# A first norm by sums and squares, a copied column pair, one more tile, stores in three parts and a new priority table in a four-layer graph kernel

## The chip, the cores and the metric

The kernel runs on one core of one Trainium2 chip. Its time is the device time of one execution in microseconds (us). The hardware profiler's span, from the first to the last instruction, stands beside it where a profile was taken. The engines are TensorE (PE: matmuls, transposes; PEld is its loading of weights, which overlaps PE), VectorE (DVE), ScalarE (ACT), GpSimd (POOL) and SyncE (SP, which here only issues DMAs).

## The reference, cut to what matters

Sixteen graphs of 1024 nodes with 128 features (float32) go through four layers. Each layer ends with `x = layernorm(x + layer(x))`.

```
x = layernorm(x + L0(x, adj))   # softmax over the mask adj^T, two weight products, two batch norms over ALL graphs
x = layernorm(x + L1(x, adj))   # h = x W + b; s1 = h a1; s2 = h a2; e = leaky_relu(s1_i + s2_j + b_a);
                                # softmax over i under the mask; relu(attention @ h)
x = layernorm(x + L2(x, adj))   # scores leaky_relu((x*a) x^T) under the mask, softmax, alpha @ x
x = layernorm(x + L3(x, adj))   # the same with other weights
```

Layer 0 needs statistics over all graphs. After that the graphs ("batches" here, 0 to 15) don't touch each other.

## The kernel before, in words

**Two stages.** The first stage streams all adjacency matrices once for the matrix products of layer 0 and its batch norms. It leaves a 128x1024 intermediate per batch in DRAM (`people`), a row sum per node (`srow`), a 128x128 matrix `m`, and two constant rows (`shift2_rows`, `row_rows`). The second stage does the rest for each batch: the end of layer 0 (called part 0), the attention layer (part 1) and the two relation layers (parts 2 and 3). After it a small check ends in a branch past a general path that isn't run.

**The second stage is a list of operations that a planner orders** (`Plan`, and `steps` from L885). A batch is a list of 389 operations (387 after the change). Each has an engine, an assumed cost, the things it reads and writes, and perhaps a tile that it takes from a class. `run` gives each operation the key `BEGIN[batch][part] + WHEN[number in the batch]`, sorts all of them by it, and places them in this order. An operation whose inputs aren't placed yet, or whose class has no free tile, is held, and goes in as soon as it can, lowest key first. The order of placing is the order of each engine's instructions. So the tables say who goes first on an engine; they are no times.

**What limits the order.** There are three lanes: batch b uses the tiles of lane b mod 3, so batch b+3 can't begin where batch b still reads. Classes: two PSUM banks (`bank`, 128x512) for transposes, small products and results; three wide PSUM tiles (`big`, 128x1024) for scores and for the accumulator of part 1; four `p`, two `e`, two `u` and two `u2` tiles in SBUF; six tiles `a` for blocks of the adjacency matrix; one `yn` and one `x0`.

**Chunks and groups.** A batch's 1024 rows are 8 chunks of 128. Row groups g0, g1, g2 hold 4, 3 and 1 chunks (`GROUPS`).

**Part 0** (L1011 to L1040): load `yn` from `people` and `x0` from `x`. DVE adds `shift2_rows` to all of `x0` (L1015, one 128x1024 instruction) and `row_rows * srow` to each chunk (L1018, eight). For each group PE transposes `yn` (L984), ACT copies it to `xt` (L997), PE multiplies by `m` into a bank (L1027), DVE adds bank and `x0` into the lane's rows (L1035, one instruction a group). `collect` then takes `bn_stats` and `bn_aggr` of each chunk on DVE (L910, L912), and `norm` computes the scale on POOL (L922, L602, L603, L924) and applies it on ACT (L928).

**Part 1**: the rows are transposed again; for 3, 3 and 2 chunks (`heads`, L1060) PE multiplies `xt` by `w1a`, which has 130 columns: h, then s1 and s2. ACT makes three exponentials from the last two columns while they are in the bank (L1064 `r`, L1068 twice into `ucol`), DVE adds the bias to h (L1071, into `hn`, which lies in the tile `q`). When all `ucol` are there, PE transposes them (L1076), ACT copies the result (L1079), SP stores it to DRAM (L1081) and loads it back, spread over all partitions, as `u` and `u2` (L1082). Eight times (j = 0..7) DVE then makes weights from `u`, `u2`, `r` (L1095) and masks and sums them (L1098), takes a reciprocal (L1102), ACT scales `hn` (L1104), PE accumulates (L1110). L1117 adds the residual and sums the row on DVE (`accum_out`), ACT squares and sums (`collect1`, L934), POOL and ACT normalize (`norm1`, L946 to L954).

**Parts 2 and 3**, for each chunk c: scores on PE into a `big` tile (L1160) and transposes of blocks done already (L1174); ACT makes two exponentials (L1182 into `q`, L1186 into an `e` tile); DVE takes the greater (L1189) and masks (L1197, L1201); PE multiplies by the rows (L1210, into a bank); DVE divides and adds (L1215, L1219); ACT squares (L961), POOL and ACT normalize (L972, L973, L977). Last, SP stores all 8 chunks of the batch by one DMA (L1228, 512 KB).

`edges` (L1006) is the load of a block of the adjacency matrix; `scores3 c`, `prod1 j` and the like below mean the scores of part 3 for chunk c, the product of part 1 for j.

Of the kernel before, what the change touches and what calls it, by code (L numbers as in the profile page):

```python
# [8 lines left out]
F32 = mybir.dt.float32  # L9
# [3 lines left out]
ALU = mybir.AluOpType  # L13
# [3 lines left out]
P = 128  # L17
# [33 lines left out]
    (0, 23570, 19046, 19887),  # L51
    (81560, 99857, 99273, 99605),
    (180283, 179933, 178976, 179336),
    (260846, 259630, 259039, 259785),
    (340425, 339643, 339400, 340684),
    (420530, 420135, 420071, 421111),
    (501099, 500913, 500796, 501932),
    (581571, 581330, 581585, 582255),
    (662316, 662119, 661973, 662851),
    (743065, 742561, 742499, 743453),  # L60
    (823698, 823225, 823027, 824059),
    (903448, 903617, 903689, 904441),
    (983901, 984234, 984054, 984182),
    (1064533, 1064511, 1063640, 1064017),
    (1145623, 1144421, 1143836, 1144698),
    (1225002, 1224181, 1224938, 1228420),
)
WHEN = (
    0, 616797, 620532, 622095, 622948, 622949, 623081, 627024, 628364, 629540, 630002, 626714,
    631822, 632733, 637162, 643567, 643568, 646286, 646287, 641291, 643860, 640736, 645808, 649097,  # L70
    651067, 652419, 650894, 651816, 622197, 623918, 623919, 635538, 637455, 638511, 638209, 638511,
    637940, 638511, 638512, 648524, 653255, 649232, 641328, 648299, 658881, 661110, 661111, 661112,
    662588, 667230, 666632, 667775, 666734, 667975, 667627, 668167, 670412, 673075, 673098, 672381,
    672546, 670025, 673246, 672675, 672066, 671126, 668971, 669586, 670331, 668972, 669567, 673463,
    673491, 673492, 676047, 679090, 680801, 664034, 688211, 689909, 692376, 693478, 693479, 687926,
    698241, 698991, 700751, 700752, 701641, 698697, 705538, 707234, 707621, 709778, 709779, 708998,
    712153, 715144, 717643, 718560, 721467, 716887, 726655, 728125, 729013, 731234, 733170, 717089,
    733625, 734320, 736822, 737034, 740401, 724366, 743419, 743865, 744720, 745329, 745637, 738233,
    746339, 748381, 750352, 751241, 751242, 757138, 760265, 754447, 757472, 756401, 757315, 759434,
    759855, 767039, 768190, 768045, 768169, 767040, 759823, 765592, 758156, 766635, 758407, 760720,  # L80
    773599, 776709, 777039, 776774, 755717, 755829, 763757, 763758, 770613, 775993, 775974, 777040,
    785094, 777064, 771978, 776750, 777256, 769200, 777666, 777741, 777742, 784114, 783251, 785781,
    786534, 787453, 791218, 791573, 800503, 779418, 782258, 784827, 784828, 785903, 787585, 788060,
    789078, 790147, 791144, 792926, 797796, 797797, 797798, 782555, 787352, 789581, 790841, 791385,
    792274, 793488, 795097, 800473, 804195, 805111, 805112, 788539, 791008, 792740, 794006, 793572,
    796652, 797265, 797266, 798162, 800436, 803200, 804120, 814202, 817329, 814870, 814589, 814203,
    791642, 794100, 796952, 796953, 796953, 799319, 799479, 800939, 806609, 809130, 809131, 814876,
    792024, 797770, 800401, 802811, 803071, 803570, 804913, 806406, 811328, 811329, 812948, 813716,
    793459, 798927, 804482, 804483, 804483, 808047, 809552, 810259, 814079, 814543, 814544, 816050,
    818957, 822320, 822707, 822318, 792793, 800025, 810709, 810918, 810710, 810919, 810920, 811403,  # L90
    815213, 816668, 818414, 818900, 820448, 823067, 817639, 818248, 819205, 822769, 824203, 823188,
    823787, 827042, 823788, 800843, 823673, 824102, 824833, 827370, 826533, 827423, 830962, 834981,
    837327, 843714, 851180, 804761, 821610, 824915, 826767, 828740, 831819, 828941, 832181, 833942,
    835127, 838612, 843863, 844088, 846801, 815635, 824848, 834898, 834899, 834899, 836257, 840309,
    840766, 840767, 846958, 848086, 852097, 822209, 824988, 836352, 838893, 838981, 841309, 845130,
    845131, 847798, 848858, 851129, 860560, 873534, 885192, 935009, 874885, 874459, 823674, 828798,
    842035, 842354, 842429, 846335, 847385, 848026, 848027, 854821, 855402, 871955, 823537, 839881,
    847114, 847115, 847497, 848712, 854653, 854822, 855246, 859637, 861054, 874928, 827895, 845561,
    848713, 854472, 854936, 855954, 857288, 858683, 859934, 865640, 867594, 875036, 878161, 933277,
    890148, 907626, 830840, 852078, 855955, 859901, 858372, 861853, 863289, 863508, 871434, 874384,  # L100
    874817, 875044, 909812, 957303, 971916,
# [453 lines left out]
def fast_path(ctx, tc, x, adj, adjt, k1, k2, w1, vecs, b_w, b_a, out, bad):  # L555
# [293 lines left out]
    class Lane:  # L849


        def __init__(self, i):
# [12 lines left out]
            self.st = tile([P, C, 6], "st")  # L865
            self.sq = tile([P, C], "sq")
            self.total = tile([P, C], "total")
            self.mv = [tile([P, C, 2], f"mv{k}") for k in range(2)]
            self.rstd = [tile([P, C], f"rstd{k}") for k in range(2)]
            self.off = [tile([P, C], f"off{k}") for k in range(2)]  # L870
            self.r = tile([P, C], "r")
            self.ucol = tile([P, 2, C], "ucol")
# [5 lines left out]
    for cls, n in (("u", 2), ("u2", 2), ("p", 4), ("e", 2)):  # L878
        plan.tiles(cls, [lanes.tile([P, N], F32, name=f"f_{cls}{i}") for i in range(n)])
# [6 lines left out]
    def steps(b):  # L886
# [20 lines left out]

        def collect(v, c):

            op(DVE, 0.2, lambda: nc.vector.bn_stats(ln.st[:, c, :], ln.rows[v][:, c, :D]),  # L910
               [key(f"rows{v}", c)], [key("st", c)], late=TAIL)
            op(DVE, 0.09, lambda: nc.vector.bn_aggr(ln.mv[v][:, c, :], ln.st[:, c, :]),  # L912
               [key("st", c)], [key(f"mv{v}", c)], late=TAIL)

        def norm(v, g):

            t, mv, rstd, off = ln.rows[v], ln.mv[v], ln.rstd[v], ln.off[v]

            def scales():
                n = len(group(g))  # L920
                neg = small.tile([P, 4], F32, name="f_ln_neg")
                nc.gpsimd.tensor_scalar(neg[:, :n], mv[:, chunks(g), 0], -1.0, 1.0, ALU.mult, ALU.mult)  # L922
                rsqrt(rstd[:, chunks(g)], mv[:, chunks(g), 1], LN_EPS, n)
                nc.gpsimd.tensor_tensor(off[:, chunks(g)], neg[:, :n], rstd[:, chunks(g)], ALU.mult)  # L924

            op(POOL, 2.0, scales, keys(f"mv{v}", group(g)), [key(f"scale{v}", g)], late=0.1)
            for c in group(g):
                op(ACT, 0.4, lambda c=c: nc.scalar.activation(  # L928
                    t[:, c, :D], t[:, c, :D], AF.Identity, bias=off[:, c:c + 1],
                    scale=rstd[:, c:c + 1]), [key(f"scale{v}", g)], [key(f"rows{v}", c)], late=TAIL)  # L930
# [72 lines left out]
        def edges(s, src):  # L1003
# [11 lines left out]
        op(DVE, 1.15, lambda t: nc.vector.tensor_tensor(  # L1015
            t, t, shift2_rows[:, None, :].to_broadcast([P, C, D]), ALU.add), mods=[x0])
        for c in range(C):
            op(DVE, 0.21, lambda t, c=c: nc.vector.scalar_tensor_tensor(  # L1018
                t[:, c, :], row_rows, srow[:, b * C + c:b * C + c + 1], t[:, c, :], ALU.mult, ALU.add),
                mods=[x0], late=TAIL if c == C - 1 else 0.0)  # L1020
        for g in range(len(GROUPS)):
            pt = turn(lambda c, t: t[:, c, :], [], g, ["xt"], args=[yn])
            copied(pt, g, ln.xt, "xt")

            def product(t, g=g):
                for k, c in enumerate(group(g)):
                    nc.tensor.matmul(t[:, k * P:(k + 1) * P], ln.xt[:, c * P:(c + 1) * P], m,  # L1027
                                     start=True, stop=True)

            pp = op(PE, 0.2235 * len(group(g)), product, [key("xt", g)], keys("rows0", group(g)),  # L1030
                    take="bank", late=0.2)

            def add(t, u, g=g, y=y):
                n = len(group(g))
                nc.vector.tensor_add(y[:, chunks(g), :D], t[:, :n * D].rearrange("p (k d) -> p k d", d=D),  # L1035
                                     u[:, chunks(g), :])

            op(DVE, 0.1 + 0.124 * len(group(g)), add, [], keys("rows0", group(g)), args=[pp, x0], late=TAIL)
            for c in group(g):
                collect(0, c)  # L1040
            norm(0, g)
# [10 lines left out]
        for c0 in range(0, C, 3):  # L1052
# [5 lines left out]
            def heads(t, c0=c0, n=n, view=view):  # L1058
# [5 lines left out]
            op(ACT, 0.15, lambda t, c0=c0, n=n, view=view: nc.scalar.activation(  # L1064
                ln.r[:, c0:c0 + n], view(t)[:, :, D], AF.Exp, bias=k0, scale=-(1 - SLOPE)),
# [237 lines left out]
```

## Time and profile before

| what | us |
|---|---|
| median of 3 runs (lowest to highest) | 1713.57 (1713.35 to 1716.01) |
| the profiled execution's own time | 1715.12 |
| its span | 1713.2 |
| PE busy in the span | 1615.4 (94%) |
| DVE busy | 1325.4 (77%) |
| ACT busy | 1071.7 (63%) |
| POOL busy | 338.3 (20%) |
| mean granted TensorE clock | 0.984 |

The profile's page gives the busy share of each engine in 40 slices of 42.8 us. The first ten slices are the first stage. Around 425 to 450 us lies the passage from the first stage to the second; from about 510 us three batches are always in work, until about 1600 us; then the last batches run out. Other views list, for one engine and a stretch of time, what it waited for, or all its instructions in order of time. A matmul of float32 shows as two records. PE's records overlap (pipelining), so a row's mean duration is longer than the pace: the 16 records of one product L1210 take 1.79 us in the chain of work.

### The profile page before, as it was taken

The numbers are of one execution on the slowest core, as the hardware profiler recorded it, in microseconds if no ns is written. First come the engines' busy times: TensorE is split into PE (matmuls) and PEld (weight loads), VectorE is DVE, ScalarE is ACT, GpSimd is POOL, SyncE is SP. The second block draws the span as 40 slices with busy tenths as digits, with TensorE's granted clock in tenths as the row PEclk, the third lists the DMA queues.
The fourth block names the chain that finished last, engine by engine and source line by source line (L and its number), as shares of the span: only waits on it lengthen the run. The fifth ranks groups of instructions, "written<-read, shape, count | busy, mean of one in ns | idle before, by whom it ended". The sixth has DMA issues, their size and how long they took to land. (4 is left out here: it accounts for less than half of the span.)

```text
span 1713.2 us, 34530 instructions
## 1 busy us (share of the span) xinstructions
PE 1615.4 (94%) x13023; PEld 1447.6 (84%) x13023; DVE 1325.4 (77%) x2940; ACT 1071.7 (63%) x2703; POOL 338.3 (20%) x615
## 2 busy tenths in 40 slices
PE   6999999999469999999999999999999999999996
PEld 3666666666469999999999999999999999999995
DVE  4665565565658989898888989898898989888764
ACT  6555555642245667767676776767677676767663
POOL 0000000000222132313313242231324232231310
PEclk9999999999789999999999999999999999999998
DMA  8999999996355757676666766766676677667551
GB/s 306 381 368 391 359 370 395 357 391 251 133 161 174 206 168 218 202 214 205 204 200 185 222 198 209 212 197 203 188 215 198 206 210 209 192 178 209 177 157 52
DMA packets 394641, 397.14 MB, mean 232 GB/s; under 512 B 10592, under 2 KB 339168, under 8 KB 394464
## 3 DMA queue, kind: packets, MB, share of 16 engines
q1 hardware_dynamic: 377824, 386.45, 69.4%
q10 hardware_dynamic: 16640, 8.39, 1.6%
q8 instruction: 104, 1.70, 0.4%
q14 instruction: 73, 0.60, 0.1%
HBM read 377.89 MB, written 16.91 MB: 230 GB/s over the span
## 5 line engine op out<-in xcount | busy, mean ns | idle before, releaser
L1210 PE MATMUL f_pbank<-f_rows,f_p 128*128 128x129 f32 x4096 | 498.9, 275 | 1.7 <-ACT f_xt L997 1.0
L1210 PEld LDWEIGHTS f_pbank<-f_rows,f_p 128*128 128x128 f32 x4096 | 478.3, 192 | 2.9 <-ACT f_xt L997 1.4
L1160 PE MATMUL f_pbig<-f_xt,f_hw 128*128 128x128 f32 x2304 | 303.9, 277 | 3.5 <-ACT f_hw L999 2.5
L1160 PEld LDWEIGHTS f_pbig<-f_xt,f_hw 128*128 128x128 f32 x2304 | 281.2, 192 | 4.8 <-ACT f_hw L999 3.0
L1110 PE MATMUL f_pbig<-f_q,f_p 128*128 128x128 f32 x2048 | 257.7, 280 | 19.0 <-ACT f_q L1104 19.0
L1189 DVE TENSOR_TENSOR f_q<-f_q,f_e 128x1024 f32<-128x1024 f32 (+7 forms) x256 | 193.4, 756 | 101.4 <-ACT f_q L1182 62.9
L1182 ACT ACTIVATE f_q<-f_pbig,f_neg_shift 128x1024 f32<-128x1024 f32 (+7 forms) x256 | 189.1, 739 | 130.3 <-PE f_pbig L1174 125.6
L1110 PEld LDWEIGHTS f_pbig<-f_q,f_p 128*128 128x128 f32 x2048 | 246.0, 197 | 21.3 <-ACT f_q L1104 20.9
L1186 ACT ACTIVATE f_e<-f_pbig,f_neg_shift 128x1024 f32<-128x1024 f32 (+7 forms) x256 | 188.4, 736 | 58.5 <-PE f_pbig L1174 53.6
L1197 DVE TENSOR_TENSOR f_p<-f_q,f_a 128x1024 f32<-128x1024 f32 (+7 forms) x256 | 192.1, 750 | 2.2 <-issue 0.2
L739 PE MATMUL f_pz<-f_xs,f_at 128*128 128x390 bf16 x1024 | 180.4, 331 | 5.0 <-DVE f_xs L722 4.2
L739 PE MATMUL f_pz<-f_zs,f_att 128*128 128x390 bf16 x1024 | 181.0, 328 | 3.1 <-DVE f_yf L742 2.9
L760 ACT ACTIVATE f_junk<-f_at,f_sq_bias 128x1024 bf16<-128x1024 int32 x128 | 146.9, 1148 | 51.6 <-DVE f_yf L742 48.2
L1095 DVE SCALAR_TENSOR_TENSOR f_p<-f_u,f_r,f_u 128x1024 f32<-128x1024 f32 x128 | 162.7, 1271 | 2.1 <-DMA f_u<-f_u_dram 2.0
L739 PEld LDWEIGHTS <-f_at 128*128 128x128 fp8e4 x1024 | 100.5, 98 | 74.1 <-issue 7.6
L739 PEld LDWEIGHTS <-f_att 128*128 128x128 fp8e4 x1024 | 100.0, 98 | 69.6 <-issue 6.5
L1098 DVE SCALAR_TENSOR_TENSOR f_p<-f_p,f_a 128x1024 f32<-128x1024 f32 x128 | 155.7, 1216 | 0.8
L1201 DVE TENSOR_TENSOR f_p<-f_pbig,f_a 128x128 f32<-128x128 f32 (+6 forms) x224 | 151.9, 678 | 0.0
L742 DVE TENSOR_REDUCE f_zr<-f_pz 128x129 f32<-128x387 f32 x128 | 63.2, 553 | 113.4 <-PE f_pz L739 113.3
L1174 PE MATMUL f_pbig<-f_ident,f_q 128*128 128x128 f32 x896 | 135.8, 274 | 3.5 <-DVE f_q L1189 3.3
L972 POOL TENSOR_SCALAR f_ln_var<-f_sq 128x3 f32<-128x3 f32 (+2 forms) x96 | 35.9, 374 | 506.1 <-ACT f_junk L961 506.1
L997 ACT COPY f_xt<-f_pbank 128x512 f32<-128x512 f32 (+2 forms) x192 | 83.2, 441 | 71.6 <-PE f_pbank L984 71.5
(165 smaller groups left out, 2075.4 us busy)
## 6 DMA issues: line engine op xcount, KB each, us to landing
f_a<-in_adjt_dram SPq DMA_DIRECT2D x384, 512.0 KB, 4.7
f_at<-in_adj_dram SPq DMA_DIRECT2D x64, 1024.0 KB, 9.1
f_att<-in_adjt_dram SPq DMA_DIRECT2D x64, 1024.0 KB, 13.5
f_u<-f_u_dram SPq DMA_DIRECT2D x32, 512.0 KB, 6.4
f_xn<-in_x_dram SPq DMA_DIRECT2D x16, 512.0 KB, 11.3
f_people<-f_yf ACTq DMA_DIRECT2D x16, 512.0 KB, 16.8
f_yn<-f_people SPq DMA_DIRECT2D x16, 512.0 KB, 3.8
f_x<-in_x_dram SPq DMA_DIRECT2D x16, 512.0 KB, 6.6
```

The lines of the kernel that those rows point to most:

```text
L739: nc.tensor.matmul(pz[:, :3 * K], a8[:, j % 2, c * 512:(c + 1) * 512:4], moving[:, j].rearrange("p k d -> p (k d)"), start=(j == 0), stop= ...
L760: nc.scalar.activation(junk, at[c // 2][:, c % 2, :], AF.Square, bias=sq_bias, accum_out=squares[:, b, c:c + 1])
L1095: p = op(DVE, 1.2, lambda e, t, t2, *_, j=j: nc.vector.scalar_tensor_tensor(e, t2, ln.r[:, j:j + 1], t, ALU.mult, ALU.max), [key("r", j)], ...
L1098: op(DVE, 1.24, lambda t, e, j=j: nc.vector.scalar_tensor_tensor(e, e, 1.0, t.rearrange("p c n -> p (c n)"), ALU.mult, ALU.mult, accum_out ...
L1110: nc.tensor.matmul(t[:, c * D:(c + 1) * D], q[:, c * P:(c + 1) * P], hn[:, j, :], start=False, stop=(j == C - 1 and c % 4 == 3))
L1160: nc.tensor.matmul(t[:, j * P:(j + 1) * P], hw[:, j * P:(j + 1) * P], xt[:, mine], start=True, stop=True)
L1182: nc.scalar.activation(q[:, blocks, :], t[:, c * P:].rearrange("p (c n) -> p c n", n=P), AF.Exp, bias=neg_shift)
L1186: nc.scalar.activation(e[:, c * P:], t[:, c * P:], AF.Exp, bias=neg_shift, scale=SLOPE)
L1189: nc.vector.tensor_max(q[:, blocks, :], q[:, blocks, :], e[:, c * P:].rearrange("p (c n) -> p c n", n=P))
L1197: nc.vector.tensor_mul(t[:, c * P:].rearrange("p (c n) -> p c n", n=P), q[:, blocks, :], k[:, c:, :])
L1201: nc.vector.tensor_mul(t[:, :c * P].rearrange("p (c n) -> p c n", n=P), s[:, :c * P].rearrange("p (c n) -> p c n", n=P), k[:, :c, :])
L1210: nc.tensor.matmul(t[:, :D + 1], w[:, j * P:(j + 1) * P], xl[:, j, :], start=(j == 0), stop=(j == C - 1))
```

## The change

It has five parts.

1. **First norm.** `collect` and `norm` are gone. In part 0 the addition of bank and `x0` is now one `scalar_tensor_tensor` per chunk with `accum_out` (the row's sum), and `collect1` and `norm1`, which part 1 used already, square and normalize. The addition of `shift2_rows` is made by group, just ahead of the group's rows.
2. **Columns of the heads.** ACT copies both columns of each `heads` bank into a new small tile `s12` (three copies), and the three exponentials are made once each from `s12` for all 8 chunks. The transpose L1076 now waits for the two whole `ucol` exponentials.
3. **Three `e` tiles** instead of two.
4. **Output by row groups**: three DMAs of 256, 192 and 64 KB per batch, each after its group is normalized.
5. **New tables** `BEGIN` and `WHEN`.

```diff
-    for cls, n in (("u", 2), ("u2", 2), ("p", 4), ("e", 2)):
+    for cls, n in (("u", 2), ("u2", 2), ("p", 4), ("e", 3)):
...
-        op(DVE, 1.15, lambda t: nc.vector.tensor_tensor(
-            t, t, shift2_rows[:, None, :].to_broadcast([P, C, D]), ALU.add), mods=[x0])
-        for c in range(C):
-            op(DVE, 0.21, lambda t, c=c: nc.vector.scalar_tensor_tensor(
-                t[:, c, :], row_rows, srow[:, b * C + c:b * C + c + 1], t[:, c, :], ALU.mult, ALU.add),
-                mods=[x0], late=TAIL if c == C - 1 else 0.0)
...
-            op(DVE, 0.1 + 0.124 * len(group(g)), add, [], keys("rows0", group(g)), args=[pp, x0], late=TAIL)
+            op(DVE, 0.07 + 0.134 * len(group(g)), lambda t, g=g: nc.vector.tensor_tensor(
+                t[:, chunks(g), :], t[:, chunks(g), :],
+                shift2_rows[:, None, :].to_broadcast([P, len(group(g)), D]), ALU.add), mods=[x0])
             for c in group(g):
-                collect(0, c)
-            norm(0, g)
+                op(DVE, 0.21, lambda t, c=c: nc.vector.scalar_tensor_tensor(
+                    t[:, c, :], row_rows, srow[:, b * C + c:b * C + c + 1], t[:, c, :], ALU.mult, ALU.add),
+                    mods=[x0], late=TAIL)
+            for k, c in enumerate(group(g)):
+                op(DVE, 0.3, lambda t, u, k=k, c=c, y=y: nc.vector.scalar_tensor_tensor(
+                    y[:, c, :D], t[:, k * P:(k + 1) * P], 1.0, u[:, c, :], ALU.mult, ALU.add,
+                    accum_out=ln.total[:, c:c + 1]), [], [key("rows0", c), key("total", c)], args=[pp, x0],
+                    late=TAIL)
+                collect1(0, c)
+            norm1(0, g)
...
-            op(ACT, 0.15, lambda t, c0=c0, n=n, view=view: nc.scalar.activation(
-                ln.r[:, c0:c0 + n], view(t)[:, :, D], AF.Exp, bias=k0, scale=-(1 - SLOPE)),
-                [], keys("r", range(c0, c0 + n)), args=[ph], late=TAIL)
-            for k in range(2):
-                op(ACT, 0.15, lambda t, k=k, c0=c0, n=n, view=view: nc.scalar.activation(
-                    ln.ucol[:, k, c0:c0 + n], view(t)[:, :, D + 1], AF.Exp, scale=SLOPE ** k),
-                    [], [key("ucol", k, c0)], args=[ph], late=TAIL)
+            op(ACT, 0.15, lambda t, c0=c0, n=n, view=view: nc.scalar.copy(
+                ln.s12[:, c0:c0 + n, :], view(t)[:, :, D:D + 2]), [], [key("s12", c0)], args=[ph], late=TAIL)
...
+        for k in range(2):
+            op(ACT, 0.15, lambda k=k: nc.scalar.activation(
+                ln.ucol[:, k, :], ln.s12[:, :, 1], AF.Exp, scale=SLOPE ** k), s12, [key("ucol", k)],
+                late=TAIL)
+        op(ACT, 0.15, lambda: nc.scalar.activation(
+            ln.r, ln.s12[:, :, 0], AF.Exp, bias=k0, scale=-(1 - SLOPE)), s12, keys("r", range(C)), late=TAIL)
...
-        op(SP, 1.5, lambda y=y: nc.sync.dma_start(out[b].rearrange("(c p) d -> p c d", p=P), y[:, :, :D]),
-           keys(f"rows{1 - v}", range(C)), late=2.0)
+        for g in every:
+            op(SP, 0.6, lambda y=y, g=g: nc.sync.dma_start(
+                out[b].rearrange("(c p) d -> p c d", p=P)[:, chunks(g), :], y[:, chunks(g), :D]),
+                keys(f"rows{1 - v}", group(g)), late=2.0)
```

From the tables, in thousands. `BEGIN` of a part grows from batch to batch by about 80.5 before and 82.4 after. The exception is the first step, from batch 0 to batch 1: part 0 goes from 81.6 to 44.4, part 1 from 76.3 to 77.2. `WHEN` of some operations:

| operation | before | after |
|---|---|---|
| load of x0 | 616.8 | 876.6 |
| yn transposes of g0, its copy, its product | 626.7, 631.8, 632.7 | 237.7, 254.6, 304.5 |
| heads for chunks 0-2, 3-5, 6-7 | 670.4, 670.0, 669.0 | 958.5, 959.0, 958.9 |
| column work: r and ucol of the three banks; after: the copies | 669 to 673 | 958.8, 961.0, 960.8 |
| after: the two ucol exponentials, r | | 961.1, 961.0, 965.1 |
| transpose of ucol | 673.5 | 961.1 |
| prod1 0, prod1 7 | 693.5, 751.2 | 983.8, 1042.6 |
| scores3 3, scores3 4 | 825.0, 828.8 | 1122.0, 1124.3 |
| output | 971.9 | 1197.8, 1245.7, 1279.7 |

## Prediction, on record before the changed kernel was run

> **What bounds the kernel now.** I read the page's slices first, then the table of stretches, then what PE waited for, then the order of time around the longest waits.
>
> ```profile
> PE   6999999999469999999999999999999999999996
> DVE  4665565565658989898888989898898989888764
> ACT  6555555642245667767676776767677676767663
> PEclk9999999999789999999999999999999999999998
> ```
>
> PE is full in the first stage (untouched) and from about 510 us on. It is hollow in the two slices from 428 to 514 us, where the granted clock falls too, and in the last. DVE runs at nine tenths beside it, ACT at seven. The stretches, columns PE, PEld, DVE, ACT, POOL, clock:
>
> ```profile
> 425.00:442.70 17.70, 8.39 (x47) 7.10 (x48) 9.76 (x43) 5.88 (x20) 4.96 (x14) 0.74 0.26 87
> 442.70:449.00 6.30, 4.99 (x23) 3.96 (x21) 1.54 (x3) 2.72 (x12) 0.00 (x0) 0.65 0.00 0
> 449.00:457.70 8.70, 3.50 (x24) 2.56 (x23) 3.42 (x9) 1.32 (x3) 0.00 (x0) 0.98 0.74 257
> 457.70:484.00 26.30, 14.61 (x85) 14.00 (x86) 21.93 (x47) 5.64 (x15) 10.55 (x12) 0.76 0.40 155
> 484.00:509.00 25.00, 15.54 (x95) 13.74 (x95) 12.11 (x33) 11.83 (x44) 6.36 (x12) 0.78 0.49 145
> ```
>
> ```profile
> 1089.00:1164.60 75.60, 74.10 (x654) 72.85 (x654) 66.67 (x158) 52.87 (x151) 21.01 (x36) 1.00 0.69 203
> ```
>
> The last line is one round of the steady part: a batch enters every 75.6 us, and PE idles 1.5 us of it. So what other engines save there is worth nothing; only PE's waits count. From 560 to 1600 us (14 rounds) they are:
>
> ```profile
> PE f_pbank L1060 <- ACT f_ucol L1068: 8.8, 14, 0.6
> PE f_pbank L1076 <- ACT f_r L1064: 8.0, 14, 0.6
> PE f_pbank L1027 <- DVE f_rows L1219: 2.7, 13, 0.2
> PE f_pbig L1160 <- DVE f_sums L1215: 0.8, 1, 0.8
> ```
>
> Together 20.3 us, and 16.8 of them belong to the heads: the third heads waits for a bank, the transpose L1076 for the exponentials. In order of time (start, duration, engine):
>
> ```profile
> 1162.05 0.17 ACT L1068 ACTIVATE f_ucol<-f_pbank 128x2 f32<-128x2 f32 x1
> 1162.26 0.42 DVE L1071 TENSOR_TENSOR f_q<-f_pbank,f_bw_row 128x256 f32<-128x256 f32 x1 [1.19 <-ACT f_ucol L1068]
> 1162.72 0.26 ACT L1064 ACTIVATE f_r<-f_pbank,f_k 128x2 f32<-128x2 f32 x1 [0.49 <-DVE f_q L1071]
> 1162.88 0.16 ACT L1068 ACTIVATE f_ucol<-f_pbank 128x2 f32<-128x2 f32 x1
> ...
> 1163.09 0.94 PE L1060 MATMUL f_pbank<-f_w1a,f_xt 128*128 128x130 f32 x6 [0.62 <-ACT f_ucol L1068]
> ...
> 1166.07 0.27 ACT L1064 ACTIVATE f_r<-f_pbank,f_k 128x3 f32<-128x3 f32 x1
> 1166.39 0.28 PE L1076 MATMUL f_pbank<-f_ident,f_ucol 128*16 128x128 f32 x1 [0.57 <-ACT f_r L1064]
> ```
>
> ACT and DVE take turns on one bank: ucol, DVE, r, ucol, 1.04 us from 1162.05 until PE may have it.
>
> **The columns of the heads.** A bank is now left after one copy and one DVE addition. The copy is not in the trace: at least 0.17 (L1068 on the same bank), at most 0.26 (L1079, a copy of 128 columns); I take 0.20, nearer to the small exponential. With the addition (0.55 for three chunks) and 0.04 between, that is 0.79 us, against 1.04. By the new table PE also has scores3 3 of an older batch (10 records, 1.12 us in the chain of waits) between the second and the third heads, where it had nothing. The order is exact only if no tile is held, so I leave 0.2 of the 0.63 us and count 0.43 a round, 14 x 0.43 = 6.0 us. The transpose waits in the end for r, 0.27 us after the last ucol; r comes after it in the new table, and the exponentials no longer take turns with DVE. PE keeps prod1 7 (1.79 us) between. I leave 0.1 of 0.57: 14 x 0.47 = 6.6 us. Both ends for the two together: 0 if ACT reaches the copies late, 16.8 if all goes. L1027's 2.7 us stay.
>
> **First norm, steady part.** DVE per batch before: L1015 19.4, L1018 40.3, L1035 24.4, L910 33.3, L912 18.7 us over 16 batches, 8.5 us. After: shift additions 1.21 plus two more starts of 0.14 (L1035: 0.687 at 512 columns, 0.551 at 384, so 0.144 fixed), 1.5; rows as before 2.5; additions with sums as L1117 with its accumulator read, (31.3 + 10.6)/16 = 2.6; in all 6.6. DVE saves 1.9 us a batch, priced at 0: it runs beside a full PE, and its own spare time is 8.9 us a round. ACT gains eight squares like L934 with accumulator read, (51.2 + 24.3)/16 = 4.7, and the heads' column work goes from (13.0 + 11.9)/16 = 1.6 to about 1.2. So ACT goes from 52.9 to 57.2 us of a round. Its spare time hides that; if the cover is gone, the price is the third rival's. POOL makes four instructions per group in either norm. The bank of L1027 is held for four additions at L1117's pace of 0.21 us instead of one of 0.69, about 0.15 more: nothing while L1027 waits only 0.2.
>
> The Trainium skill (VectorE: DVE Perf Modes, the section on the TRN2 errata) speaks against this part: each DVE instruction pays 58 cycles with an SBUF source, 120 with a PSUM one, so it wants tiles of 512 elements or more. As an estimate by that page, five more PSUM starts and two more SBUF starts would cost DVE 0.75 us a batch; the trace's 0.144 us a start says 1.0. Either is on an engine that does not end the round, and the sum stays.
>
> **New waits of the new order.** Every engine's order changes, which no row prices. In the steady part the bounds are no new wait, and about 2 us a round, ACT's excess below. The waits of today's order are the nearest rows (0.2 us apiece for L1027), so I charge 0.2 a round, 2.8 us. Steady part: -6.0 - 6.6 + 2.8 = **-10 us**.
>
> **Passage between the stages.** Batch 0 is alone. Today DVE ends part 0 at 438, POOL and ACT normalize until 442.7, L1076 runs at 448.8, `u` is back and L1095 begins at 457.7. After: shift_rows is ready at 430.6; g0 needs half a shift addition (0.6), four rows (1.1), four additions, so its squares start near 432.7 and end after four at L934's pace of 0.53, near 434.9; POOL needs 1.8, apply four times 0.4. The groups follow each other at ACT's pace, and I get the last apply near 440.7, 2 us earlier, and L1076 about 3 us earlier with the shorter column work. Second: the load of x0 for batch 1 is issued at 449.8 today, behind the store of `ucol`, and DVE waits 5.6 us for it. In the new table it stands ahead of that store, as soon as x0 is free near 438. So batch 1's part 0 falls into DVE's idle 449 to 454, where today it lies among batch 0's eight L1095/L1098 pairs: 26.3 us from 457.7 to 484, of which the pairs need 8 x 2.7 = 21.6. That frees up to 4.7 us. Together 7.7; batch 1's own trip through DRAM (L1076 at 494.5) still lies behind, so I take 6. Ends: 0, and 13 if the hollow stretch at 484 to 509 shrinks as well. Passage: **-6 us**.
>
> **Third e tile.** In the steady part L1186 waits for PE only, never for an e tile; DVE waits for exponentials 69 us there, which is DVE's time. Price 0. At most it lets ACT run ahead, which is part of the new order.
>
> **Output by groups.** Two more issues of about 0.5 us on SP, which waits most of the time; but a store that waits for ACT holds the loads queued behind it. Six tiles `a` cover that: in the steady part no PE wait names a DMA. At the end the last store is issued at 1703.4 and SP waits for it until 1709.1, but PE's branch also takes from 1704.1 to 1708.9. So a faster store gains at most 0.2 us; price 0. The Trainium skill (DMA: Bandwidth & Descriptors, section Bandwidth) says to batch to 1 MiB and that under 64 KB descriptors dominate, which speaks against the split. By that page's fixed 2.0 us plus bytes over 436 GB/s the 64 KB would take an estimated 2.2 us against 3.2. The trace has 3.9 us for the 512 KB at the end, and the branch hides the difference.
>
> **Sum.** -10 - 6 = -16 us. The profiled execution took 1715.1 (span 1713.2 plus 1.9); less 16 it is 1699.1. The median of the runs lies 1.5 lower, 1713.6, so the forecast for the median is **1697.6 us**.
>
> **Rivals.**
> - *All waits vanish.* PE loses its 20.3 us of steady waits and the passage gives 13: 1713.6 - 33 = 1680. For it: the waits sit in one place of the code. Against: L1027's and the new order's own.
> - *Waits only move.* The heads' 12.6 us come back elsewhere in the round, and the passage gives 0 to 6: 1708 to 1714. For it: DVE at 88% leaves little room for any fixed order.
> - *ACT becomes late, and the kernel slower.* The squares of part 0 fall, by the table, at the end of part 2 of the batch two ahead, where ACT already has that batch's squares and applies. Transposes of part 3 wait for those applies, and PE is in order. From 1139.4 to 1149.5 ACT has 7.5 us busy of 10.1, so 2.6 spare, and gets 4.7: 2.1 us late. It decides from the point where PE's next instruction needs an apply within those 2.1 us. If all of it reaches PE, 14 x 2.1 = 29 us; less 6 of the passage, +23: 1737. Half of it: +9, 1722. Against: PE has matmuls of two other batches to put between.
> - *The copies do nothing*, because ACT, held by exponentials of 1.1 us, reaches them late; this is the second rival's cause too and is counted there.
>
> **Chances.** Forecast (1687 to 1708) 0.54; all waits vanish (below 1687) 0.13; waits only move (1708 to 1717) 0.13; ACT late (above 1717) 0.20. About 0.2%, 3.4 us, is what a measurement can tell from no change. From the cases: faster by more than that 0.72 (all of the first two, and 0.05 of the third), within it 0.08, slower 0.20. The range leaves out about 0.08 below and 0.11 above: 1682 to 1722. Forecast's own range: 1687 to 1708.
>
> **What would show it.** Right: PE's waits at L1060 and L1076 in the steady part fall from 16.8 us to about 4; a round takes 74.9 us; DVE's busy time falls by some 30 us and ACT's grows by some 70; L1095 begins near 455 and the full part some 6 us earlier. Wrong: PE waits for ACT's applies (L954, L977) or DVE for exponentials more than today; a round longer than 75.6; a passage that still ends at 509.

## The result and the profile after

| what | before | after |
|---|---|---|
| median of the runs (us) | 1713.49 | 1691.62 (1690.43 to 1692.32) |
| ratio, 95% interval | | 0.9868 (0.9851 to 0.9885) |
| profiled execution, its span (us) | 1715.12, 1713.2 | 1691.56, 1689.7 |
| PE, DVE, ACT, POOL busy (us) | 1615.4, 1325.4, 1071.7, 338.3 | 1608.6, 1306.2, 1122.9, 361.2 |

The changed kernel is 21.9 us faster (1.3%). The forecast was 1697.6. Code lines moved up: L1060 (heads) is now L1039, L1071 (their addition) L1045, L1076 (transpose of ucol) L1057, L984 (the other transposes) L964, L1027 (the product of part 0) L1001. The copy of the columns is L1043. The slices of the page after:

```profile
PE   6999999999569999999999999999999999999996
DVE  4565565565367889898988989898898989898775
ACT  6555555552446777778677777877777787777575
PEclk9999999999579999999999999999999999999999
```

The passage is still two hollow slices wide and its clock is lower than before (5 and 7 for 7 and 8). The end has no dip. One round of the steady part, from one transpose of ucol to the next (columns as in the stretches above):

```profile
1083.19:1157.62 74.43, 73.54 (x653) 72.63 (x652) 65.62 (x157) 55.74 (x161) 22.07 (x36) 1.00 0.70 206
```

PE's waits from 560 to 1580 us (total, times, longest):

```profile
PE f_pbank L1039 <- DVE f_q L1045: 8.1, 13, 0.6
PE f_pbank L1001 <- DVE f_rows L1200: 2.7, 13, 0.2
PE f_pbig L1141 <- DVE f_sums L1196: 0.3, 1, 0.3
```

The transpose of ucol waits no more (8.0 us before). The wait of the third heads is as long as it was; another engine ends it. The order of time there:

```profile
1153.15 1.28 PE L1039 MATMUL f_pbank<-f_w1a,f_xt 128*128 128x130 f32 x10
1153.35 1.01 ACT L1163 ACTIVATE f_q<-f_pbig,f_neg_shift 128x896 f32<-128x896 f32 x1 [1.18 <-PE f_pbig L1155]
...
1154.26 0.16 ACT L1043 COPY f_s<-f_pbank 128x6 f32<-128x6 f32 x1
1154.44 0.56 DVE L1045 TENSOR_TENSOR f_q<-f_pbank,f_bw_row 128x384 f32<-128x384 f32 x1 [0.72 <-ACT f_s L1043]
...
1155.06 0.94 PE L1039 MATMUL f_pbank<-f_w1a,f_xt 128*128 128x130 f32 x6 [0.63 <-DVE f_q L1045]
1155.11 0.40 ACT L1085 ACTIVATE f_q<-f_q,f_sums 128x128 f32<-128x128 f32 x1 [0.69 <-DVE f_sums L1083]
...
1155.83 1.95 PE L1091 MATMUL f_pbig<-f_q,f_p 128*128 128x128 f32 x16
```

ACT reaches the copy only after an exponential of 1.01 us; DVE's addition waits 0.72 us for the copy, and the bank comes free with the addition. The addition starts 0.02 us after the copy's end, though both only read: it waits for the copy's signal. The Trainium skill (PSUM — Partial Sum Buffer, section "PSUM bank collisions raise a hardware error") says that two engines must be kept apart on one bank, reads against reads too; the wait in this row agrees.

**Where the time went.** The starts of the transposes of ucol mark the batches. Batch 2's is 2.0 us earlier than before (562.17 for 564.13), and 1.1 of that is there when the first stage ends (`shift_rows` is ready at 429.5 for 430.6). That stage is unchanged, and over all the traces here its end lies between 429.5 and 431.1, so this part is chance. From batch 2 to 15, 13 rounds, 967.8 us take the place of 979.5: **-11.7**. From batch 15's to the end of the span it is 159.8 for 169.6: **-9.8**. Together 23.5 us, the difference of the spans.

### The profile page after: what moved, and what is told of

It is laid out like the page before. It is cut to its first block, busy times and chain, and to the rows that moved or that the text cites. A ratio compares the mean times of both kernels' runs of the same rounds, so it can differ in the third digit from the quotient of the medians.

```text
span 1689.7 us, 34809 instructions
## 1 busy us (share of the span) xinstructions
PE 1608.6 (95%) x13007; PEld 1443.5 (85%) x13023; DVE 1306.2 (77%) x2924; ACT 1122.9 (66%) x2911; POOL 361.2 (21%) x615
## 5 line engine op out<-in xcount | busy, mean ns | idle before, releaser
L1076 DVE SCALAR_TENSOR_TENSOR f_p<-f_u,f_r,f_u 128x1024 f32<-128x1024 f32 x128 | 163.3, 1276 | 6.4 <-DMA f_u<-f_u_dram 6.4
L952 POOL TENSOR_SCALAR f_ln_var<-f_sq 128x1 f32<-128x1 f32 (+2 forms) x96 | 38.5, 401 | 500.3 <-ACT f_junk L941 500.3
L914 ACT ACTIVATE f_junk<-f_rows,f_total 128x128 f32<-128x128 f32 x256 | 102.7, 401 | 15.2 <-DVE f_rows L1015 5.1
```

The costliest lines, as they stand in the source:

```text
L1076: p = op(DVE, 1.2, lambda e, t, t2, *_, j=j: nc.vector.scalar_tensor_tensor(e, t2, ln.r[:, j:j + 1], t, ALU.mult, ALU.max), [key("r", j)], ...
```

## The experiments

In the lists of keys a line names the operation and its key, in thousands. The ratios set each run against the kernel before, timed again beside it. Its median went from 1713.5 to 1716.2 us between these groups, so a difference between medians of two groups is good to about 2 us.

**Code or table.** The changed code in the old order:

```diff
-WHEN, BEGIN: new tables
+WHEN, BEGIN: old tables, operations matched by what they do
```

> The changed code in the old order: every operation that both kernels have keeps its old key, a new one gets the key of the operation that it replaces. Theory A (the code frees PE: the transpose of ucol no longer waits for r and for the turns of ACT and DVE on one bank): 1700 us or less, and PE's wait at the transpose of ucol in the steady part under 2 us of the former 8. Theory B (the new table frees PE, the code only makes such an order possible): 1708 to 1725 us, the transpose still waits, and other waits come up where the new operations have no good place in the old order.

Measured 1805.63 us, ratio 1.0539 (1.0517 to 1.0561); a round takes 82.2 us. PE waits most for ACT's apply of the first norm (39.8 us in 13 waits), ahead of the last transpose before the heads: the new square of the last chunk starts 10 us after its addition. The transpose of ucol waits no more, as Theory A had it.

The old code in the new order:

```diff
-WHEN, BEGIN: old tables
+WHEN, BEGIN: new tables, operations matched by what they do
```

> The old code in the new order: shared operations take the new keys; the statistics of a chunk take the key of its square, r and ucol of a bank that of its copy, the store that of the last group. Theory A: the three exponentials and DVE still take turns on a bank, so both of the heads' waits stay (some 16 us in the steady part), and the time is 1705 us or more. Theory B: most of the gain is there without the code, 1700 us or less, and the transpose of ucol waits under 2 us.

Measured 1792.29 us, 1.0449 (1.0432 to 1.0466); a round takes 80.8 us, and PE waits 29.3 us in 17 waits for DVE's addition of part 0. Here too the transpose of ucol waits no more, as Theory B had it. Both theories, as put, fall, since the loss lies elsewhere. Neither half has a gain of its own to keep: with an order made for other code the kernel loses 77 to 90 us. So the parts are tried one by one below, with the rest of one kernel in place.

**The third e tile and the stores.** The changed kernel with two `e` tiles:

```diff
-("e", 3)
+("e", 2)
```

> The changed kernel with two tiles of exponentials instead of three, nothing else. The recorded prediction priced the third tile at 0: within 2 us of the changed kernel's 1691.6. Rival: the new order lets ACT run a tile ahead and counts on it, then ACT is held by DVE's maximum, PE gets its masked tiles later, and the time is 3 to 12 us longer.

Measured 1692.32 us, 0.9872 (0.9855 to 0.9888): nothing, as forecast. With one store of 512 KB:

```diff
-        for g in every:
-            op(SP, 0.6, ... out[b] ... [:, chunks(g), :] ...)
+        op(SP, 1.5, ... out[b] ... y[:, :, :D] ...)
```

> The changed kernel with one store of 512 KB per batch instead of three. The recorded prediction priced the split at 0 to 0.2 us, since PE's branch would take as long: 1691.5 to 1692.0. Rival: what stands at the end is SP's wait for the landing of the last store; then the time is 2 to 3 us longer, 1693.6 to 1694.6, and all of it lies behind the cast of the check's result (from there to the end 9.8 us as before, and 7.5 with three stores).

Measured 1693.65 us, 0.9874 (0.9858 to 0.9891), 2.0 us more by the medians. The trace puts only about 0.5 of it at the end: from the check's cast until the closing semaphores begin it takes 6.5 us with one store, 6.0 with three, 6.4 before. The rest lies between the transposes of batch 1 and batch 2 (72.1 us for 69.8), where the two kernels are alike. From run to run this step differed by over two us without a change near it. So the rival's range was met by chance: its reason asked for all of the time behind the cast.

**The columns.** The changed kernel with the old column work, three exponentials a bank, r last:

```diff
-            op(ACT, ... nc.scalar.copy(ln.s12 ...))
+            for k in range(2):
+                op(ACT, ... ln.ucol[:, k, c0:c0 + n], ... AF.Exp ...)
+            op(ACT, ... ln.r[:, c0:c0 + n], ... AF.Exp ...)
...
-            ln.ucol[:, k, :], ln.s12[:, :, 1], AF.Exp ...
-            ln.r, ln.s12[:, :, 0], AF.Exp ...
```

> The changed kernel with the old column work: per bank of the heads three exponentials straight from the bank (the two ucol, then r), no s12; each takes the key of the copy that it replaces, all else stays. Theory A (the copies themselves give the steady part its gain: the stretch of PE from the first heads to the transpose of ucol took 5.50 us a round before and takes 4.46 now): the stretch is near 5.5 again, some 14 x 1.0 us, 1702 to 1706 us. Theory C (it is the order: r after both ucol, ACT's and DVE's turns on the bank in a better order): the stretch stays under 4.8 and the time within 4 us of 1691.6.

Measured 1696.72 us, 0.9894 (0.9873 to 0.9916). The stretch from the first heads to the transpose is 4.69 us, in all rounds. So of 1.03 us between before (5.49) and after (4.47) the copies are worth 0.22; the rest stays without them. All of the 0.22 lies between the first and the third heads, where the whole gain is 0.29. Theory C holds for the stretch. The time is 5.1 us longer and not within 4: 2.9 are 13 rounds of 0.22, and 2.6 more are there at batch 2, behind the step that differs from run to run.

Then the same order in the kernel before, code untouched:

```
operation                          key before            key here
two ucol and r of chunks 6 and 7   669.0, 670.3, 669.6   669.0, 669.0, 669.0
two ucol and r of chunks 3 to 5    672.1, 672.7, 673.2   672.1, 672.1, 672.1
two ucol and r of chunks 0 to 2    672.4, 673.1, 673.1   672.4, 672.4, 672.4
```

> The kernel before with one change in the table: in each bank of the heads ACT makes both ucol exponentials and then r in one go, where it took turns with DVE's addition. No code is changed. Theory C (most of the steady gain is the order of these few instructions, which the copies are not needed for): PE's stretch from the first heads to the transpose of ucol falls from 5.50 us to about 4.7, and the time by 14 x 0.8 = 11 us, 1701 to 1705 us. Theory A (it needs the copies): 5.2 us or more of stretch, and 1710 us or more.

Measured 1707.26 us, 0.996 (0.9946 to 0.9974). The stretch falls to 4.61 us, as Theory C said; the transpose's wait is gone, and that of the heads is left:

```profile
PE f_pbank L1060 <- DVE f_q L1071: 6.8, 14, 0.5
```

The round falls only from 75.34 to 74.79 us: 0.33 of the 0.88 come back elsewhere in the round, and the time lies between the two theories' ranges. So an order of nine instructions, in the old code, gives 0.55 us a round where the whole change gave 0.90. What else is new, code and table together, has some 0.35 left.

**The first norm.** The changed kernel with the old statistics:

```diff
-                op(DVE, 0.3, ... scalar_tensor_tensor ... accum_out=ln.total ...)
-                collect1(0, c)
-            norm1(0, g)
+            op(DVE, ..., add, ...)
+            for c in group(g):
+                collect(0, c)
+            norm(0, g)
```

> The changed kernel with the old first norm of part 0: one DVE addition of bank and x0 per group, bn_stats and bn_aggr on DVE at the places of the squares, the old scale on POOL; shift and rows by group, columns, e tiles, stores and table stay. The recorded prediction priced the first norm at 0 in the steady part (DVE 1.9 us a batch less, ACT 4.4 us more, both beside a full PE): within 3 us of the changed kernel's 1691.6. Rival: DVE is the engine behind PE's small waits, its longer part 0 comes back on PE, and the time is 5 us or more longer.

Measured 1722.62 us, 1.0054 (1.0037 to 1.007): 31 us more than the changed kernel. A round takes 76.48 us, 2.05 more, and DVE's busy time in it is 67.98 instead of 65.54 us. By the order of PE's instructions all of the 2.05 us come between 39 and 61 us into the round. There, first in the changed kernel, then in this one (DVE is the third engine):

```profile
1047.76:1069.76 22.00, 21.79 (x195) 21.55 (x195) 20.12 (x62) 16.71 (x60) 10.43 (x18) 1.00 0.78 233
```

```profile
1063.45:1087.45 24.00, 22.49 (x195) 21.57 (x195) 22.04 (x63) 13.71 (x46) 12.65 (x17) 1.00 0.70 209
```

PE has the same 195 matmuls. DVE has 1.92 us more to do and had 1.88 idle, yet the stretch grows by 2 and DVE is idle as long as before (1.96 of 24): its idle time was waiting, not room. The largest of PE's new waits names DVE:

```profile
PE f_pbig L1164 <- DVE f_sums L1219: 9.5, 11, 0.9
```

In the new order the shorter DVE work is needed, as far as this run tells: it can't tell the length of the old statistics from the places that they got in an order made for the squares. Nor does it make the new norm worth 29 us against the kernel before: the old norm in its own order (the run with the columns' order) has rounds of 74.79.

**The remaining wait of the heads.** First by putting PE work ahead of it:

```
operation             key after   key here
heads of chunks 3-5   959.0       960.7   (behind prod1 7 of the batch ahead)
transpose of ucol     961.1       963.4   (behind the next product of part 3)
```

> The changed kernel with another order around the heads: the third heads go behind the last product of part 1 of the batch ahead, and the transpose of ucol behind the next product of part 3. The remaining wait of the third heads for their bank (0.62 us a round, ended by DVE's addition, 8.1 us in all) gets 1.79 us of PE work in front of it. If that wait is a true loss of PE: 8 us less, 1683 to 1685 us, and the row of waits at the heads under 1 us. Rival: it moves to the next product or to the transpose, and the time stays within 2 us of 1691.6.

Measured 1710.24 us, 0.9968 (0.9954 to 0.9983): 19 us longer, and both guesses were wrong. The heads' row is gone, and two others lead the list (lines are 5 lower: L1086 is prod1, L1136 the scores):

```profile
PE f_pbig L1086 <- ACT f_q L1080: 15.8, 14, 1.1
PE f_pbig L1136 <- DVE f_p L1177: 4.9, 14, 0.4
```

prod1 7 needs a scaling by ACT, which needs a reciprocal that DVE makes behind the addition to the heads (the rows at 1155.11 above). While PE did the third heads, this chain was hidden. Second by bringing the copy forward:

```
operation                                  key after      key here
heads of chunks 6-7, their copy            958.9, 960.8   958.5, 958.5
heads of chunks 0-2, their copy            958.5, 958.8   958.6, 960.8
additions for chunks 6-7, 0-2              960.8, 959.2   959.2, 960.1
first exponential of part 3, chunk 1       1121.4         1122.1  (now behind the copy)
reciprocal of prod1 7                      1042.6         1041.1  (now ahead of the additions)
```

> The changed kernel with a few other keys: the heads of two chunks come first again, ACT copies their columns ahead of the exponential of part 3 chunk 1 (0.9 us, behind which the copy stands now) and the reciprocal of the last product of part 1 goes ahead of the addition to the heads. If the remaining wait of the third heads (0.62 us a round) comes from the copy's place behind that exponential: the row falls under 0.2 us a round, the round from 74.43 to about 73.9, and the time is 6 to 9 us less, 1683 to 1686 us. Rival: the exponential, then 0.6 us later, holds up DVE's maximum and the next product of part 3, and the time stays within 2 us of 1691.6 or is longer.

Measured 1688.10 us, 0.9849 (0.9833 to 0.9866), 3.5 less. The heads don't wait:

```profile
1151.25 2.26 PE L1034 MATMUL f_pbank<-f_w1a,f_xt 128*128 128x130 f32 x16
...
1151.89 0.16 ACT L1038 COPY f_s<-f_pbank 128x4 f32<-128x4 f32 x1 [1.63 <-PE f_pbank L1034]
1151.95 1.01 ACT L1158 ACTIVATE f_q<-f_pbig,f_neg_shift 128x896 f32<-128x896 f32 x1
```

The stretch is 3.95 us and the round 74.08, 0.35 less of the 0.52 that the stretch lost. The copy now starts just ahead of the exponential, and the wait is gone, so it came from the copy's place as far as these moves together tell; the first bank is also smaller now. The other half of the expected gain is given back in the round (0.17) and at the end (161.3 us after the last transpose for 159.8), where the clock fell (see **The end**).

**The passage.** The changed kernel with batch 1's part 0 held back:

```diff
             key.append(BEGIN[op[0]][op[8]] + WHEN[k])
+            if op[0] == 1 and op[8] == 0 and k > 1:
+                key[-1] = max(key[-1], 960430)
```

> The changed kernel with part 0 of batch 1 held back, on all engines but SP, until the transpose of ucol of batch 0 is placed. Theory D (in the passage PE, which works in order, stands at batch 1's transposes of yn until 437.9 and DVE at batch 1's x0 until 447.9, and both hold up batch 0): the transpose of ucol of batch 0 starts near 449 instead of 455.3, the first weights of part 1 near 456.5 instead of 462.7, and the time is 3 to 6 us shorter, 1686 to 1689 us. Rival: what batch 1 loses by it is paid back while DVE makes batch 0's weights, and the time is within 2 us of 1691.6.

Measured 1688.55 us, 0.9844 (0.9825 to 0.9862), 3.1 less. Batch 0's transpose starts at 447.98, batch 1's at 486.34 for 492.42, batch 2's 4.0 us earlier; the rounds are the same. Theory D holds, at the lower end. What stands in the way in the changed kernel:

```profile
437.91 1.09 PE L964 MATMUL f_pbank<-f_ident,f_yn 128*128 128x128 f32 x4 [3.52 <-DMA f_yn<-f_people]
439.72 2.47 PE L1001 MATMUL f_pbank<-f_m,f_xt 128*128 128x128 f32 x10 [0.72 <-issue]
...
447.91 0.69 DVE L1007 TENSOR_TENSOR f_x<-f_x,f_shift_rows 128x512 f32<-128x512 f32 x1 [5.38 <-DMA f_x<-in_x_dram]
...
455.27 0.37 PE L1057 MATMUL f_pbank<-f_ident,f_ucol 128*16 128x128 f32 x1 [0.94 <-DVE f_q L1045]
```

PE stands at batch 1's transposes, which wait for `yn` until 437.91, and batch 0's last product of part 0 is among the ten records behind them. DVE stands at batch 1's `x0` until 447.91, with batch 0's additions to the heads behind it; but that cost nothing here, since DVE is done with `x0` at 449.2 and then waits for the first heads and their copy until 450.11. So of Theory D's two places it is PE's that the trace shows. The clock of this stretch, first before, then after the change:

```profile
445.00:465.00 20.00, 9.97 (x55) 8.46 (x53) 12.16 (x29) 3.11 (x13) 2.40 (x2) 0.78 0.37 132
```

```profile
445.00:465.00 20.00, 9.98 (x35) 6.92 (x34) 8.51 (x28) 6.72 (x26) 3.28 (x8) 0.50 0.49 185
```

**The end.** The kernel before, part 3 of batch 15 in the new order (`LAST` holds the new table's keys of part 3):

```diff
+            if op[0] == 15 and op[8] == 3 and k < 388:
+                key[-1] = LAST[...]
```

> The kernel before with one change: part 3 of the last batch follows the new table, so that its transposes for chunk 1 come ahead of the scores for chunk 3. Theory E (the order of the drained last part: 3.02 us of PE idle there, after which the granted clock is 0.54 and 0.61 in two stretches of 4 us): the hole is under 2 us, the clock stays at 1.0, and the time is 3 to 5 us less than before, 1708.5 to 1710.5 us. Rival: the last part is set by ACT and DVE, its order costs nothing, and the time is within 1.5 us of 1713.5.

Measured 1712.71 us, 0.9986 (0.9976 to 0.9997): 2.4 us by the ratio, 3.6 by the trace from the last transpose of ucol. Two stretches after the hole, first before, then here (the clock is the third number from the end):

```profile
1675.61:1679.61 4.00, 2.79 (x13) 2.79 (x14) 2.94 (x4) 1.72 (x3) 0.00 (x0) 0.54 0.50 146
1679.61:1683.61 4.00, 4.00 (x25) 4.00 (x24) 1.78 (x4) 0.59 (x1) 0.00 (x0) 0.61 0.40 116
```

```profile
1675.19:1679.19 4.00, 2.57 (x23) 2.58 (x24) 2.87 (x4) 1.94 (x3) 0.00 (x0) 1.00 0.49 137
1679.19:1683.19 4.00, 4.00 (x37) 3.89 (x37) 3.69 (x8) 1.69 (x3) 0.00 (x0) 1.00 0.44 125
```

Theory E holds in this trace, with a correction. PE's idle time isn't shorter: one hole of 3.02 us became two of 1.24 and 1.90, and the transposes behind them start at the same time after the batch's transpose of ucol (133.4 us for 133.2). But the clock stays at 1.00. The next 16 records take 1.8 us instead of 3.4, the next 8 0.9 instead of 1.7: 2.5 of the 3.8 us until the last product.

The clock isn't sure to stay, though. Eleven of the traces have the holes of 1.24 and 1.90 us at this place, and in five of them it is halved behind the holes for 3.41 us. So it is in the run with the copy first:

```profile
1653.03:1656.44 3.41, 1.51 (x15) 1.28 (x14) 2.27 (x3) 1.86 (x3) 0.00 (x0) 1.00 0.52 144
1656.44:1659.85 3.41, 3.41 (x18) 3.41 (x17) 2.38 (x6) 1.22 (x2) 0.00 (x0) 0.50 0.51 143
```

There the 16 records take 2.8 us and the next 8 1.5: 1.6 us more, which is all of its longer end. The other three traces have one hole of 3.0 us, and the clock is halved behind it in each. So the new order made the fall rarer, and that the changed kernel and this run were spared it is in part luck.

**Both orders together.**

```diff
+keys of the run with the copy first
+keys of the run with batch 1 held back
```

> The changed kernel with both orders that were faster alone: batch 1's part 0 held back behind batch 0's transpose of ucol (3.1 us less alone) and the columns of the heads copied ahead of the exponential (3.5 us less alone). If the two places don't touch each other, as one lies in the passage and the other in the steady part, the savings add: 6.6 us less than 1691.6, 1685.0 us (1683.5 to 1686.5), with rounds of 74.08 and batch 0's transpose at 448. Rival: the longer last part that the second of them had (161.3 us from the last transpose to the end, against 159.8) grows, and the time is no better than 1687.

Measured 1682.29 us (1679.61 to 1683.15), 0.9812 (0.9799 to 0.9826). This is the fastest version, 9.3 us under the changed kernel. It is 2.7 better than the sum of the two. The surplus is there at batch 2's transpose (555.9 us, for 558.2 with batch 1 held back alone), behind the step that differs from run to run, and why isn't settled. The rounds are the 74.08 of the run with the copy first.

## Why the prediction was right, and where not

The sum was -16 and the result -22; the time lies in the forecast's own range. The steady part (-10, measured -11.7) was right for about the reason given. That the total fits as well is luck: of the 6 us of the passage less than 1 came, and the end gave 9.8 that had no term.

- **Columns of the heads (-6.0 and -6.6).** The total was right, the split wrong. The transpose lost its whole wait, 0.57 us a round, with 0.17 of small gaps beside it; I had left 0.1. The third heads kept their wait of 0.62, which was to be 0.2. Still the stretch from the first to the third heads is 0.29 shorter, by a stall that lies inside the rows and has no entry among the waits. Together 1.03 a round. The price of the copy was fair (0.163 measured, 0.20 taken). What failed is the step from the copy to the bank: I counted 0.79 us from the moment ACT starts, and ACT starts late, behind an exponential. The scores that the table puts between the second and the third heads didn't come there: they start 5 us behind the third heads (10 records at 1159.94), so they were held, as I had allowed.
- **The reason behind it** was half wrong. I put the gain of the heads down to the copy, and that of the transpose to the copy and to r's place. The runs give it 0.22 of 1.03; the rest is that r no longer stands between the bank and the transpose and that ACT and DVE no longer take turns, which the old code can have by its table alone (0.88).
- **New waits, 0.2 a round.** The stretch gained 1.03 and the round 0.90, so 0.13 was given back.
- **First norm, priced at 0.** DVE's work is 26.8 us shorter by its rows (30 forecast; the page's total fell by 19), ACT's squares 75.7 longer. As the difference between two orders the zero isn't contradicted, but its reason is: "its own spare time is 8.9 us a round" is an average. In the new order DVE has 1.9 us spare in a stretch of 22, and the old norm there costs 2.05 a round. The old norm's cost in an order tuned around the new squares wasn't visible in the old trace; what the new norm would give with the old order alone stays open. The Trainium skill's rule on small instructions (VectorE: DVE Perf Modes, the section on the TRN2 errata) was no reason against the part: the total of DVE fell.
- **Passage, -6.** Wrong: about -0.9 beside the first stage's own 1.1. I had the load of x0 early and batch 1's part 0 in DVE's idle time, and both came (the load at 442.6 for 449.8). But I never followed the key of the yn transposes, 237.7 in the table, through PE's queue: it puts batch 1's first transposes ahead of batch 0's last product. The first weights of part 1 began at 462.7, not 455; the clock from 445 to 465 was 0.50 for 0.78 before. Batch 1's gain (its transpose 2.1 us earlier) paid that back. With batch 1 held back batch 0's transpose came at 448.0, where I had put it near 446.
- **Third e tile, 0.** Right: 0.7 us, within the spread.
- **Output by groups, at most 0.2.** Near: 0.4 to 0.5 by the trace. "PE's branch also takes until 1708.9" took its length as fixed. It was 4.81 us before, 4.31 with one store in the new kernel and 3.79 with three. The last 64 KB landed after 1.9 us; the estimate by the Trainium skill's DMA: Bandwidth & Descriptors, whose figure is for DMAs that GpSimd issues, was 2.2.
- **The end, not priced.** -9.8 us: 3.1 because part 3 begins earlier after the last transpose of ucol (no run tells why), 4.5 in part 3, of which the run with its new order alone has 3.8, and 2.3 behind the cast. Of these 2.3 only 0.4 stand before the closing semaphores; the closing itself takes 1.6 us for 3.5. It is short in every run of the changed code, with one store, two `e` tiles, the old columns or the old norm too, and 3.5 to 4.0 in every run of the old code. So no one of these parts makes it, and its cause is open.
- **Signs.** The waits at the heads and at the transpose fell from 16.8 to 8.1 us, not to 4. A round is 74.43 us (74.9 forecast); DVE's busy time fell by 19 (30), ACT's rose by 51 (70). The clock was back at full at 509.0, for 508.6 before, so the sign named for a wrong passage came.
- **Rivals.** PE has no wait for ACT's applies in the steady part, so "ACT becomes late" didn't come; with the old order it did (39.8 us). The last rival's reason, that ACT reaches the copies late, is what kept the third heads' wait. "All waits vanish" (1680) is what the last run of the experiments comes near, with L1001's 2.7 us and 0.3 at the scores left of its rows.

## What to carry to other kernels

An order made by hand belongs to its code: exchanged whole they lost 77 to 90 us, while a few keys moved in either kernel gained. Before rewriting an instruction try moving it, since nine keys gave more here than the new copies. Spare time of an engine counts in the stretch where the work falls, not over a round. A key that says "as early as possible" puts an instruction at the head of an in-order queue, where it waits for its DMA with everything behind it; follow each such key through the first batches too.

## What the hardware did that I had not expected

- **The clock goes by steps of its own.** In all fourteen traces it changes only at whole multiples of 3.41 us after its first change. Every step at full clock that was followed by half clock had PE busy for 0.57 of it or less, every one that was followed by full clock for 0.45 or more; back to full it went only after a step with 0.82 or more. So it matters how a hole lies in the steps: PE was busy for 1.30 of 3.41 us in the step with most of the hole of 3.02, and the clock fell; with the two shorter holes it was busy for 1.55 in the run with part 3 alone in the new order, and the clock stayed, for 1.51 in the run with the copy first, and it fell. The Trainium skill (TensorE: Matmul & The Clock Gate, Part 1: The HAM clock gate) has a free-running window of 3.4 us, and half speed after an idle one. The steps and the halves fit the traces, but the window needn't be idle. Between 0.45 and 0.57 both outcomes occur, so the busy share of these records isn't the whole rule.
- **Small stalls hide in the rows.** PE's records overlap, so gaps of 0.2 to 0.3 us had no entry among the waits; only start to start showed them.
- **A store's size shows at the end only a little:** the last stores of 64, 192 and 256 KB landed in 1.9, 2.1 and 2.4 us, those of 512 KB in 3.9 to 4.8, but the end moved by about 0.5 us.
